# Half of the last part's q rows come through GpSimd gathers with an add instead of TensorE one-hot products

## The chip, the cores and the metric

The kernel runs on 1 core of one Trainium2 chip. The metric is the device time of one execution in microseconds (us), lower is better. Besides the plain runs, one execution was recorded by the hardware profiler; line numbers (L1119) are lines of the kernel before unless the text says otherwise.

## What is computed

A graph attention layer with 12,500 nodes of 128 values and 412,500 edges, with a norm around it. Each edge has a source, a target and 64 features:

```python
attn_in = jnp.concatenate([q[src], k[tgt], eh], axis=-1)
hmid = jax.nn.leaky_relu(attn_in @ A1 + b1, SLOPE)
scores = jax.nn.leaky_relu(hmid @ A2 + b2, SLOPE)
w = jax.nn.softmax(scores.mean(axis=-1), axis=0)      # over all edges
out = jax.ops.segment_sum(w[:, None] * v[tgt], src, num_segments=num_nodes)
y = h + out                                            # then two layer norms, with x added between
```

`q`, `k`, `v`, `h` are linear in the node features and `eh` in the edge features. `attn_in @ A1` is a sum of three terms, so the q, k and edge terms can be multiplied by A1 beforehand and added per edge.

## The kernel before

The edges come sorted by target, and the sums go by source. So the kernel sorts by itself. The 98 blocks of 128 sources each have a region in a DRAM table `rtab`, and the edges are worked through in six parts, one after the other.

*Records.* `make(p)` takes groups of 1024 edges. TensorE adds the k and v rows of the target (one-hot products with a window of `kvtab`) and the edge term in PSUM; ScalarE copies them into `rec`, a record of 260 fp32 values: 128 of k plus edge term, 128 of v, and the source's number in its block. GpSimd scatters the records, 128 rows an instruction, to the rows of `rtab` that were counted out for their blocks (L907, an indirect DMA behind a nop). This gives 3224 scatters in all.

*Sums.* `sums_of` (from L1004) works through units. A unit is two blocks, in the last part 2 x 7 = 14 tiles of 128 records, so that part has 49 units. For each unit:

- `load` (L1041): SP brings the records from `rtab` into `rt`, 1820 KB in the last four parts. There are six such buffers.
- `sources` (L1063): VectorE takes the source numbers of the records as `sl`, with the rows past the block's end masked to -1e30.
- `turn`, `turned`, `put`, `spread` (L1071, L1078, L1085, L1090): TensorE turns `sl`, VectorE makes it 8 bits (`slT`), SP writes it to DRAM (`row`) and reads it back spread to all partitions (`rowB`, 224 KB). SP's queue is in order, so it stands until `row` has landed.
- `onehot` (L1099): VectorE compares `rowB` with the partition's number: `ohT`, four tiles at a time.
- `hidden` (L1110, L1119): TensorE transposes the k rows of four tiles into the PSUM tile `ph` and adds to them the q rows of the sources, as three products (the q table `qtab` is kept as three bf16 pieces, `load_q`, L1052) with `ohT`. A unit of 14 tiles has 14 transposes and, since a chunk of four may straddle two blocks, 5 pieces x 3 = 15 products.
- `sloped`, `leaky` (L1130, L1134): ScalarE and VectorE make the leaky ReLU into `hm`; then `scores`, `heads` and the maximum follow on TensorE, and `weights` (L1219) on ScalarE.
- `select` (L1228) and `weigh` (L1242): VectorE compares `sl` with a row of block numbers, four tiles at a time (`ohs`, bf16), and ScalarE scales each tile by the edges' weights (`ohw`, fp32, two buffers).
- `add` (L1271): TensorE multiplies `ohw` with the v rows, two passes a tile, and sums over the unit's block. `total` and `store` put the block's sum beside the older parts' sums.

*The order* is written out by hand. For each unit a loop lays down a start step `s0`, a step for the load (when a buffer is free, and at least `lead` steps ahead) and, from there, the step of each function; a unit takes 8 steps. The functions of a step are issued in that order, each to its engine's queue, and each engine works in order. The sums of part p run between the steps of `make(p + 1)`; the last part's have nothing beside them. There `closing` (from L1339) already adds `beta` to the rows of `x` (`rows_x`, `moved` on GpSimd at L1357, `put_x`: 14 groups of 7 blocks). After the last unit `closing` makes the two norms, group by group.

*Tables.* In the first part `tables` (from L1502) makes `kvtab`, `qtab` and `htab` (the fp32 rows of h) between the groups: TensorE multiplies, VectorE adds the bias, ScalarE and VectorE split the sum into bf16 pieces, `own` (L1560) copies h, and `put` (L1579, L1580) writes them, 14 groups of 7 blocks.

## Time and profile before

| | |
|---|---|
| three runs | 4999.63, 5000.75 and 5002.16 us, median 5000.75 |
| profiled execution | 4997.18 us, of which the span from its first to its last instruction is 4995.4 |
| busy, share of the span | PE 84%, PEld 62%, VectorE (DVE) 80%, ScalarE (ACT) 65%, GpSimd (POOL) 66% |
| mean granted TensorE clock | 0.906 |
| moved by DMA | 1505.5 MB, mean 301 GB/s |

PE is TensorE's matmuls and PEld its weight loads, which overlap. A row of a group names line, engine and operation, the tiles written and read with their sizes and the count, then the busy time in us and the mean of one in ns, then the idle time of the engine just before them and what ended it. A row of a timeline begins with start and duration in us; in brackets at its end is the idle time ahead of it. SPq is SP issuing a DMA, not its transfer. Busy time of matmuls is modelled and neighbours overlap, so starts tell more than durations there.

### The profile page before, as it was taken

What the parts mean: (1) busy time and instruction counts of PE and PEld (TensorE: products, weight loads), DVE (VectorE), ACT (ScalarE), POOL (GpSimd) and SP (SyncE); (2) the same over time, 40 slices, a digit from 0 to 9 for tenths busy, and PEclk for the clock granted to TensorE, in tenths of its full rate; (3) what the DMA queues carried; (4) which work ended last, traced back from release to release, by engine and by line L of the source; (5) the groups of instructions that cost most, each with busy time, mean ns of one, the idle gap of its engine ahead of it and who ended that gap; (6) DMA issues with size and microseconds to landing.
All of it is one profiled execution on the core that took longest, in us unless ns stands there. A gap on an engine that the chain in (4) does not pass through costs nothing.

```text
span 4995.4 us, 98371 instructions
## 1 busy us (share of the span) xinstructions
PE 4185.0 (84%) x32676; PEld 3106.9 (62%) x32676; DVE 3984.1 (80%) x10117; ACT 3260.1 (65%) x8686; POOL 3315.9 (66%) x3268
## 2 busy tenths in 40 slices
PE   5665488898888888899999899999899999899980
PEld 3443366676566666577676676676677766667760
DVE  8886477788777777788888888888888888677778
ACT  3433266666566666677677677777777777677876
POOL 5777777777777777777777777777777777310002
PEclk7776588899999999999999899999999999999995
DMA  8999699998999988899899898989899999788763
GB/s 287 360 349 347 237 327 340 347 301 269 307 322 334 324 294 289 281 318 310 309 307 311 297 322 313 311 305 314 285 329 313 321 318 309 251 291 278 263 224 142
DMA packets 604241, 1505.50 MB, mean 301 GB/s; under 512 B 103587, under 2 KB 315702, under 8 KB 601929
## 3 DMA queue, kind: packets, MB, share of 16 engines
q1 hardware_dynamic: 448681, 1069.47, 64.9%
q0 software_dynamic: 154752, 429.39, 22.7%
q8 instruction: 259, 4.24, 0.3%
q14 instruction: 261, 2.14, 0.1%
q10 hardware_dynamic: 288, 0.26, 0.0%
HBM read 929.49 MB, written 608.37 MB: 308 GB/s over the span
## 4 chain that ended last, share of the span: by engine, by line
DMA 35%; PE 23%; DVE 15%; POOL 12%; issue 7%; ACT 6%; SPq 1%; ACTq 0%; DVEq 0%; POOLq 0%
DMA rtab<-rec,idx 17%; POOL rtab L907 12%; DMA rt<-rtab 8%; PE psm L1271 6%; DMA row<-slT 4%; PE ph L1119 4%; DMA rowB<-row 3%; PE pkv L884 3%; PE ph L1110 3%; ACT rec L895 2%; PE psc L1147 2%; DVE hm L1134 2%; PE pkv L878 2%; ACT ohw L1242 2%; PE psm L1180 2%
## 5 line engine op out<-in xcount | busy, mean ns | idle before, releaser
L907 POOL DMA_INDIRECT rtab<-rec,idx x3224 | 3253.2, 1009 | 1046.2 <-issue 778.6
L895 ACT ACTIVATE rec<-pkv 128x1024 f32<-128x1024 f32 x806 | 821.9, 1020 | 876.0 <-DMA rtab<-rec,idx 550.4
L1242 ACT ACTIVATE ohw<-ohs,w 128x128 f32<-128x128 bf16 x3822 | 1258.4, 399 | 44.7 <-DVE ohs L1228 34.3
L1271 PE MATMUL psm<-rt,ohw 128*128 128x128 f32 x7644 | 1160.2, 294 | 9.7 <-ACT ohw L1242 9.3
L1271 PEld LDWEIGHTS psm<-rt,ohw 128*128 128x128 f32 x7644 | 999.1, 200 | 58.7 <-ACT ohw L1242 16.8
L1130 ACT ACTIVATE hm<-ph 128x512 f32<-128x512 f32 (+1 forms) x1078 | 581.5, 539 | 403.9 <-PE ph L1119 399.8
L1119 PE MATMUL ph<-ohT,qs 128*128 128x256 bf16 (+3 forms) x4116 | 819.7, 321 | 0.0
L878 PE MATMUL pkv<-kvs,ohd 128*128 128x256 bf16 x3224 | 532.0, 292 | 263.4 <-ACT rec L895 252.8
L1134 DVE TENSOR_TENSOR hm<-ph,hm 128x512 f32<-128x512 f32 (+1 forms) x1078 | 668.4, 620 | 102.6 <-ACT hm L1130 101.4
L1110 PE MATMUL ph<-ident,rt 128*128 128x128 f32 x3822 | 628.1, 283 | 44.5 <-DVE hm L1134 43.2
L884 PE MATMUL pkv<-WeS,eat 64*128 64x128 f32 x6448 | 635.6, 320 | 0.0
L884 PEld LDWEIGHTS pkv<-WeS,eat 64*128 64x128 f32 x6448 | 469.8, 205 | 191.7 <-issue 187.3
L1099 DVE TENSOR_SCALAR ohT<-rowB,iotaP 128x512 bf16<-128x512 uint8 (+1 forms) x1078 | 518.7, 481 | 85.4 <-DMA rowB<-row 80.6
L878 PEld LDWEIGHTS <-ohd 128*128 128x128 bf16 x3224 | 317.1, 103 | 388.0 <-issue 298.2
L1110 PEld LDWEIGHTS ph<-ident,rt 128*128 128x128 f32 x3822 | 472.5, 152 | 62.0 <-DVE hm L1134 51.2
L1228 DVE TENSOR_TENSOR ohs<-iotaE,sl 128x512 bf16<-128x512 bf16 (+1 forms) x1078 | 430.0, 399 | 68.3 <-ACT ohw L1242 66.4
L1119 PEld LDWEIGHTS <-qs 128*128 128x128 bf16 x4116 | 396.0, 100 | 128.7 <-issue 5.1
L847 DVE TENSOR_TENSOR ats<-pc,oh 128x792 f32<-128x792 f32 x403 | 392.2, 973 | 86.6 <-PE pc L829 82.7
L1180 PE MATMUL psm<-headsum,z 128*128 128x4 f32 (+1 forms) x2156 | 285.7, 254 | 135.7 <-DVE part L1287 88.3
L1147 PE MATMUL psc<-hm,A2s 128*32 128x512 f32 (+3 forms) x2352 | 341.1, 545 | 65.7 <-DVE slT L1078 62.1
L858 DVE TENSOR_REDUCE pos<-ats 128x8 f32<-128x792 f32 x403 | 390.0, 968 | 4.0
L1180 PEld LDWEIGHTS psm<-headsum,z 128*128 128x128 f32 (+1 forms) x2156 | 280.0, 201 | 156.8 <-DVE part L1287 105.9
(175 smaller groups left out, 4082.3 us busy)
## 6 DMA issues: line engine op xcount, KB each, us to landing
rt<-rtab SPq DMA_DIRECT2D x196, 1820.0 KB
eat<-in_ea SPq DMA_DIRECT2D x201, 512.0 KB
rt<-rtab SPq DMA_DIRECT2D x49, 1560.0 KB
rt<-rtab SPq DMA_DIRECT2D x49, 1300.0 KB
qs<-qtab SPq DMA_DIRECT2D x294, 192.0 KB
rtab<-rec,idx POOLq DMA_INDIRECT x3224
dstb<-dtab SPq DMA_DIRECT2D x201, 256.0 KB
rtab<-empty SPq DMA_DIRECT2D x98, 520.0 KB
```

What stands on the lines that cost most here:

```text
L878: nc.tensor.matmul(pk[:, h, i, :], ohd[:, t * P : (t + 1) * P], kvs, start=(i == 0), stop=False,)
L884: nc.tensor.matmul(pk[:, h, i, :D], eat[h * DE : (h + 1) * DE, (j + i) * P : (j + i + 1) * P], WeS[h * DE : (h + 1) * DE, :], start=False, ...
L895: nc.scalar.activation(rec[:, :, :, : 2 * D], pk, AF.Copy)
L907: one_tile = nc.gpsimd.indirect_dma_start(out=rtab[p % TABS][:, :], out_offset=bass.IndirectOffsetOnAxis(ap=idxs[g][:, t : t + 1], axis=0) ...
L1099: nc.vector.tensor_scalar(st["oh"][k][:, : n * P], st["rowB"][:, t0 * P : (t0 + n) * P], iotaP, None, op0=ALU.is_equal,)
L1110: nc.tensor.matmul(ph[:, j * P : (j + 1) * P], st["rt"][:, t0 + j, :D], ident, is_transpose=True, start=(j == 0), stop=False,)
L1119: nc.tensor.matmul(ph[:, cols], st["qs"][:, j0 // t, s, :], oh[:, cols], start=False, stop=(s == 2 and j1 == t0 + n),)
L1130: nc.scalar.activation(hm, state[i]["ph", k][:, : n * P], AF.Copy, scale=SLOPE)
L1134: nc.vector.tensor_tensor(hm, ph[:, : n * P], hm, op=ALU.max)
L1180: nc.tensor.matmul(st["psS"][:, t0 + j : t0 + j + (nv - 1) * sw + 1 : sw], z[: 32 * nv, j * P : (j + 1) * P], headsum[: 32 * nv, :nv], sta ...
L1242: nc.scalar.activation(ohw[:, j, :], ohs[:, :, j], AF.Copy, scale=st["w"][:, t0 + j : t0 + j + 1])
L1271: nc.tensor.matmul(st["psS"][:, (1 + u) * P : (2 + u) * P], ohw[:, j, :], st["rt"][:, t0 + j, D : 2 * D], start=(k == 0), stop=(k == t - 1),)
```

## The change

In every second unit of the last part (`drawn`: 24 of the 49) the q rows are not multiplied in. VectorE clamps the source numbers to 0..127 and adds the block's first row, once per block (`rows_of`). Then GpSimd issues, tile by tile, an indirect DMA that gathers 128 rows of 512 bytes from a new DRAM table `q32` of fp32 q rows and adds them onto the k part of the records in SBUF (`draw`, 14 per unit). `hidden` only transposes. In these units `turn`, `turned`, `put`, `spread`, `load_q` and `onehot` are gone, `sources` stays five steps behind the load and the gathers come one step later; `lead` is longer by two steps. For the third four tiles of a drawn unit VectorE makes `ohw` in one operation a tile from the record's source number and the weight, in place of one `select` and four `weigh` on ScalarE. In all groups `moved` goes from GpSimd to VectorE. In the first part `own` copies q and h out of PSUM, and `put` writes `q32` in addition (448 KB a group).

```diff
+    q32 = dram.tile([nb * P, D], FP, name="q32")
...
+    first_last = NU - sum(p == NP - 1 for p, _, _ in units)
+    drawn = {i for i in range(first_last, NU) if (i - first_last) % 2 and units[i][2] <= GT}
...
             lead = turn + 8 if p in starts or p == 0 else turn + 8 + LATE
+            lead += 2 * (i in drawn)
...
+        def rows_of(i):
+            st, (p, bs, t) = state[i], units[i]
+            near = scp.tile([P, TM], FP, name="S")
+            nc.vector.tensor_scalar(
+                near[:, : len(bs) * t], st["sl"][:, : len(bs) * t], 0.0, P - 1.0,
+                op0=ALU.max, op1=ALU.min,
+            )
+            st["at"] = []
+            for u, b in enumerate(bs):
+                idx = ixp.tile([P, GT], I32, name="idx")
+                nc.vector.tensor_scalar(
+                    idx[:, :t], near[:, u * t : (u + 1) * t], float(b * P), None, op0=ALU.add
+                )
+                st["at"].append(idx)
+
+        def draw(i):
+            st, (p, bs, t) = state[i], units[i]
+            for k in range(len(bs) * t):
+                nc.gpsimd.indirect_dma_start(
+                    out=st["rt"][:, k, :D], out_offset=None, in_=q32[:, :],
+                    in_offset=bass.IndirectOffsetOnAxis(
+                        ap=st["at"][k // t][:, k % t : k % t + 1], axis=0
+                    ),
+                    compute_op=ALU.add,
+                )
...
         def hidden(i, t0, c, n, k):
-            oh = st["oh"].pop(k)
+            oh = st["oh"].pop(k, None)
...
-                    is_transpose=True, start=(j == 0), stop=False,
+                    is_transpose=True, start=(j == 0), stop=(oh is None and j == n - 1),
...
-            while j0 < t0 + n:
+            while oh is not None and j0 < t0 + n:
...
         def select(i, t0, n):
+            if i in drawn and t0 == 8:
+                ohw = st["sel"][t0] = selp.tile([P, 4, P], FP, name="ohw")
+                for j in range(n):
+                    nc.vector.tensor_scalar(
+                        ohw[:, j, :], iotaE[:, :, j], st["rt"][:, t0 + j, 2 * D : 2 * D + 1],
+                        st["w"][:, t0 + j : t0 + j + 1], op0=ALU.is_equal, op1=ALU.mult,
+                    )
+                return
...
         def weigh(i, t0, n):
+            if i in drawn and t0 == 8:
+                return
...
             do(load_at, load, i)
-            do(s0 - turn_at - 2 - e, sources, i)
-            do(s0 - turn_at, turn, i)
-            do(s0 - turn_at + 1 + e, turned, i)
-            do(s0 - turn_at + 1 + e, put, i)
-            do(s0 - turn_at + 3 + 2 * e, spread, i)
-            do(s0 - 9, load_q, i)
+            if i in drawn:
+                do(load_at + 5, sources, i)
+                do(load_at + 5, rows_of, i)
+                do(load_at + 6, draw, i)
+            else:
+...
...
-                do(s - 1 - e, onehot, i, c, n, k)
+                if i not in drawn:
+                    do(s - 1 - e, onehot, i, c, n, k)
...
         def moved(g):
-            nc.gpsimd.tensor_add(three(t, 0), three(t, 0), wide(t[:, NB * D : NB * D + D]))
+            nc.vector.tensor_add(three(t, 0), three(t, 0), wide(t[:, NB * D : NB * D + D]))
...
-                    job["h"] = np_.tile([P, NB, D], FP, name=f"h{job['i'] % 2}")
+                    job["h"] = np_.tile([P, NB, 2, D], FP, name=f"h{job['i'] % 2}")
...
         def own(job, b, m):
-            nc.scalar.activation(job["h"][:, b : b + m, :], job["ph", b][:, :, 1, :], AF.Copy)
+            nc.scalar.activation(job["h"][:, b : b + m, :, :], job["ph", b], AF.Copy)
...
-                nc.sync.dma_start(out=htab[:, bl, :], in_=job["h"])
+                nc.sync.dma_start(out=htab[:, bl, :], in_=job["h"][:, :, 1, :])
+                nc.sync.dma_start(
+                    out=q32.rearrange("(b p) d -> p b d", p=P)[:, bl, :], in_=job["h"][:, :, 0, :]
+                )
```

More of the change, by code (lines that the diff above doesn't have):

```diff
@@ L1007, in sums_of @@
         plans, s0, first, free, done, starts, ends = [], 19, None, [], [], {}, {}
-        for p, bs, t in units:
+        for i, (p, bs, t) in enumerate(units):
             nt = len(bs) * t
@@ L1299, in sums_of @@
             do(load_at, load, i)
-            do(s0 - turn_at - 2 - e, sources, i)
-            do(s0 - turn_at, turn, i)
-            do(s0 - turn_at + 1 + e, turned, i)
-            do(s0 - turn_at + 1 + e, put, i)
-            do(s0 - turn_at + 3 + 2 * e, spread, i)
-            do(s0 - 9, load_q, i)
+            if i in drawn:
[3 more added lines that the diff above has]
+            else:
+                do(s0 - turn_at - 2 - e, sources, i)
+                do(s0 - turn_at, turn, i)
+                do(s0 - turn_at + 1 + e, turned, i)
+                do(s0 - turn_at + 1 + e, put, i)
+                do(s0 - turn_at + 3 + 2 * e, spread, i)
+                do(s0 - 9, load_q, i)
             for k in range(nk):
```

## The prediction

> **What bounds the kernel now.** I began with the stages: the last scatter on GpSimd in the timeline, and the windows view, whose columns are the stretch, its length, then the busy time of PE, PEld, DVE, ACT and POOL, the granted clock, the DMA share and GB/s.
>
> ```profile
> 4302.80 0.96 POOL L907 DMA_INDIRECT rtab<-rec,idx  x1 [0.30 <-issue]
> ```
>
> ```profile
> 4313.00:4576.00 263.00, 241.31 (x1789) 181.96 (x1790) 193.49 (x520) 190.67 (x561) 29.92 (x14) 0.98 0.83 286
> 4576.00:4840.00 264.00, 262.75 (x2045) 201.62 (x2044) 203.90 (x587) 218.17 (x648) 0.00 (x0) 1.00 0.69 240
> ```
>
> GpSimd's last scatter ends at 4303.8, and the 49 units of the last part run from about 4313 to 4840, alone on the core. I call the first stretch early (the rows of x pass through it) and the second late. Late, TensorE is busy 262.75 of 264 us and ScalarE 83%, VectorE 77%, GpSimd 0. That says TensorE, but two other loops have to be read first, since they are what is left when TensorE gets less. The load of the records is issued by SP (L1041) and first read by VectorE (L1063). Here are the first and the last load of 22 in each stretch, with their reads:
>
> ```profile
> 4335.35 0.38 SPq L1041 DMA_DIRECT2D rt<-rtab  x1
> 4344.95 0.18 DVE L1063 SCALAR_TENSOR_TENSOR sl<-mask,rt 128x14 bf16<-128x14 bf16 x1 [1.77 <-DMA rt<-rtab]
> 4567.41 0.39 SPq L1041 DMA_DIRECT2D rt<-rtab  x1
> 4576.52 0.18 DVE L1063 SCALAR_TENSOR_TENSOR sl<-mask,rt 128x14 bf16<-128x14 bf16 x1 [1.15 <-DMA rt<-rtab]
> 4578.53 0.37 SPq L1041 DMA_DIRECT2D rt<-rtab  x1
> 4585.94 0.18 DVE L1063 SCALAR_TENSOR_TENSOR sl<-mask,rt 128x14 bf16<-128x14 bf16 x1 [1.09 <-DMA rt<-rtab]
> 4784.74 0.37 SPq L1041 DMA_DIRECT2D rt<-rtab  x1
> 4792.37 0.19 DVE L1063 SCALAR_TENSOR_TENSOR sl<-mask,rt 128x14 bf16<-128x14 bf16 x1 [1.33 <-DMA rt<-rtab]
> ```
>
> A unit takes (4567.41 - 4335.35)/21 = 11.05 us early and (4784.74 - 4578.53)/21 = 9.82 us late; a load takes 9.6 to 9.1 us early and 7.4 to 7.6 late, until VectorE has it. VectorE waits for it in every unit. The waits view (us in total, times, longest), the first row late, the others early:
>
> ```profile
> DVE sl L1063 <- DMA rt<-rtab: 31.7, 25, 2.2
> DVE sl L1063 <- DMA rt<-rtab: 34.1, 21, 3.0
> DVE ohT L1099 <- DMA rowB<-row: 22.3, 18, 2.9
> PE ph L1110 <- DVE hm L1134: 16.0, 15, 2.2
> ```
>
> Late, TensorE never waits for VectorE, so it is the bound. Early it does: VectorE stands behind the records, behind the source rows spread over the partitions (rowB), and behind GpSimd, as the part on VectorE shows. So the early stretch is bound by waits and the late one by TensorE, with the load close behind.
>
> **The change part by part.** *TensorE.* A unit of 14 tiles has five pieces of three products (15 matmuls, L1119) and one turn (L1071). One late unit in the timeline of PE:
>
> ```profile
> 4650.09 0.49 PE L1119 MATMUL ph<-ohT,qs 128*128 128x256 bf16 x3
> 4650.41 1.06 PE L1271 MATMUL psm<-rt,ohw 128*128 128x128 f32 x8
> 4651.90 0.81 PE L1119 MATMUL ph<-ohT,qs 128*128 128x512 bf16 x3
> 4652.64 1.06 PE L1147 MATMUL psc<-hm,A2s 128*32 128x512 f32 x8
> 4655.28 0.82 PE L1119 MATMUL ph<-ohT,qs 128*128 128x384 bf16 x6
> 4655.94 0.66 PE L1271 MATMUL psm<-rt,ohw 128*128 128x128 f32 x4
> 4656.87 0.81 PE L1119 MATMUL ph<-ohT,qs 128*128 128x512 bf16 x3
> 4657.61 0.22 PE L1071 MATMUL psc<-identB,sl 128*14 128x128 bf16 x1
> 4657.77 1.28 PE L1271 MATMUL psm<-rt,ohw 128*128 128x128 f32 x8
> ```
>
> Busy times overlap, so I go by start to next start: 0.32 + 0.74 + 0.66 + 0.74 for the products and 0.16 for the turn, 2.62 us. A drawn unit costs TensorE 9.82 - 2.62 = 7.20, and the mean of two units is 8.51. If nothing else came to bind, that is 1.31 us a unit.
>
> *GpSimd.* It gets 24 x 14 = 336 gathers with an add in the last part. No accumulating DMA stands in the trace; the nearest rows are the scatters of records (the group, then two starts in a row):
>
> ```profile
> L907 POOL DMA_INDIRECT rtab<-rec,idx x3224 | 3253.2, 1009 | 1046.2 <-issue 778.6
> 4195.75 1.03 POOL L907 DMA_INDIRECT rtab<-rec,idx  x1 [0.30 <-issue]
> 4197.09 0.96 POOL L907 DMA_INDIRECT rtab<-rec,idx  x1 [0.30 <-issue]
> ```
>
> 0.96 and 0.30 of issue are 1.27 us each, 17.8 us for a drawn unit and so 8.9 us a unit for a pair: more than TensorE's 8.51. The bounds of one gather are 0.96 (no gap, since the nop ahead of each scatter is not there) and 1.92 + 0.30 (all of it twice, if a row is fetched from two places); I take 1.27, the same number of rows in the same kind of instruction. The upper end, 31 us a pair, would cost over 250 us; the range leaves it out. By the Trainium skill, *DMA: Bandwidth & Descriptors*, "Anatomy of one DMA", many descriptors can be made before their number costs anything; by that rule the second fetch is free and the sum stays at 17.8, but no run here shows it. A gather waits for its load and its index; behind it in POOL's queue stand only later gathers, and then the closing adds. A drawn unit's products are 15 steps after its first gather, about 18 us, and the last tile is needed 6 steps later: 17.8 us and a landing fit.
>
> *The load beside the gathers.* In the late stretch the DMA engines move this much in slices of 5 us:
>
> ```profile
> GB/s 396 139 388 114 391 168 376 148 365 110 392 188 338 111 392 189 337 164 349 184 331 197 317 224 302 242 280 259 243 287 238 298 196 285 256 296 233 289 192 300
> ```
>
> They reach 390 while a load runs and fall to 110 between loads, so there is room, though not where the load is. Its 1820 KB (1.86 MB) take 4.8 of its 7.6 us at that rate. Gathers of 64 KB every 1.27 us are 52 GB/s, 13%: 0.7 us more. Half the units lose their q table and rowB (192 and 224 KB, 1.1 us at 390), 0.5 us less on average. The load becomes 7.8 us late; early, where 6.5 of 9.35 us are transfer, 9.35 + 1.0 - 0.5 = 9.85. What it bounds: the read and the slope behind it on VectorE (0.10 and 0.68) have to be over when TensorE comes to the transposes that follow the next load's issue, so a unit is not shorter than the load and 0.9 us: 8.7 late, 10.7 early.
>
> *VectorE and ScalarE.* The move of `moved` is worth more than its size. One GpSimd add of x rows, the VectorE instruction beside it, the group of that instruction late, and an operation of the added size:
>
> ```profile
> 4458.49 2.09 POOL L1357 TENSOR_TENSOR rec<-rec 128x896 f32<-128x896 f32 x1 [15.53 <-DMA rec<-in_beta]
> 4458.71 2.15 DVE L1228 TENSOR_TENSOR ohs<-iotaE,sl 128x512 bf16<-128x512 bf16 x1
> L1228 DVE TENSOR_TENSOR ohs<-iotaE,sl 128x512 bf16<-128x512 bf16 x62 | 26.1, 422 | 14.0 <-ACT ohw L1242 13.9
> L1472 DVE TENSOR_TENSOR rt<-rt,eat x14: 1057/1059/1093, 4861.4 to 4976.3; 128x896 f32<-128x896 f32 x14
> ```
>
> While GpSimd added, VectorE took 2.15 for 0.42. That stall (1.7) goes 14 times, and 1.06 us of work comes in, about 9 us less in all; the new add makes VectorE wait if the x rows are late, 0 to 2 us each. A drawn unit takes from VectorE four one-hots, the turned row and one select, and adds the clamp, two indices and four weighed one-hots:
>
> ```profile
> L1099 DVE TENSOR_SCALAR ohT<-rowB,iotaP 128x512 bf16<-128x512 uint8 x62 | 29.7, 479 | 3.7 <-DMA rowB<-row 3.7
> L1099 DVE TENSOR_SCALAR ohT<-rowB,iotaP 128x256 bf16<-128x256 uint8 x20 | 7.1, 353 | 0.3
> L1078 DVE TENSOR_SCALAR slT<-psc 14x128 uint8<-14x128 f32 x21 | 5.7, 269 | 0.0
> L1242 ACT ACTIVATE ohw<-ohs,w 128x128 f32<-128x128 bf16 x288 | 94.8, 398 | 0.6
> ```
>
> Away: 3 x 0.48 + 0.35 + 0.27 + 0.42 = 2.48. Added: three of the size of L1063 (0.18) and four of 128x128, between that and 0.35; I take 0.27: 1.6 us. VectorE gets shorter, to about 7.1 a unit, and ScalarE loses four of L1242, 0.33 each: neither becomes the bound. One new wait is real: these four write a buffer that TensorE's adds of the same step release, so VectorE stands behind TensorE, with the slope behind it, for 0 to 1 us a drawn unit; I take 0.2, 4 us in all.
>
> *SP.* Three DMAs a drawn unit go, and with them SP's wait for the row to come back; the early wait for rowB (22.3 us) halves. The plan puts two more steps between load and use; the order gets 7 steps longer, which holds no work.
>
> *The first part* writes the fp32 q rows too: 14 x 448 KB, 6.4 MB, and the copy out of PSUM doubles in size.
>
> ```profile
> 60.00:480.00 420.00, 262.19 (x1427) 174.76 (x1426) 340.22 (x746) 170.98 (x395) 311.14 (x314) 0.74 1.02 352
> 480.00:600.00 120.00, 58.53 (x343) 39.06 (x343) 63.42 (x153) 32.07 (x70) 91.09 (x91) 0.56 0.69 240
> ACT sp L1557 <- DMA qtab<-sp: 71.9, 11, 11.0
> ```
>
> There the DMA is full (1.02, 352 GB/s), so the writes are 18 us of transfer. But GpSimd sets the pace: a scatter every 1.34 us full, against 1.32 when the share is 0.69, though ScalarE stood 71.9 us behind such writes. So full DMA costs it little; between 0 and 18 I take 4.
>
> *Sum.* Late, the largest of 8.51, 8.9 and 8.7 is 8.9: 0.92 x 27 units = 25. Early 10.7: 0.35 x 24 = 8. Back come 4 and 4. That leaves 25 us. The profiled execution took 4997.2 us for a span of 4995.4, and the runs shown have a median of 5000.75; 25 off is 4972 for the one and **4976** for the other.
>
> **The rivals.** *TensorE's bound is reached* (gathers issue faster than 1.21 and the load isn't slowed): late 1.31 x 27 = 35, early as much as the wait for rowB and GpSimd's stall allow, 24: less 4, 4946. For it: the holes of 110 GB/s. Against it: the load waits of 31.7.
>
> *Every added row is fetched twice*, from the table and from the record. Then gathers take 103 of 390 GB/s, and the late transfer of 4.8 us becomes 6.5: load 7.6 + 1.7 - 0.5 = 8.8, bound 9.7, nothing gained. Early 6.5 us become 8.9: load 11.2, bound 12.1, 1 us x 24 lost. With 8 for the rest: 5030. The Trainium skill, *Collectives: The Full Stack*, "The bandwidth ceiling", has it that a reducing DMA is half as fast because it has two source reads. No run here shows an adding DMA.
>
> *The other side: GpSimd becomes the bound.* It decides from 19.64/14 = 1.40 us a gather, where a drawn unit's gathers last as long as two units do now; 0.13 us above the scatters. At 1.7 us (half of 0.96 more, for the second list of fetches) a pair takes 23.8: late 4.2 x 13.5 = 57, early 1.7 x 12 = 20, with 4 for the tables 5082. For it: POOL's total is within 10% of a pair already. Against: over 3224 scatters the mean is 1009 ns, with VectorE busy 340 of 420 us beside some of them, so little is added to an issue.
>
> *It gives nothing:* the products go, and VectorE's waits for load, x rows and adds take the time back; 5001.
>
> **How the numbers follow.** Chances: forecast 0.35, TensorE's bound 0.20, nothing 0.10, fetched twice 0.15, GpSimd 0.20. Within 0.2% is 10 us, about what a measurement of this kernel can tell from no change. Faster 0.55, same 0.10, slower 0.35. The range goes down to 4935, somewhat below TensorE's bound, and up to 5065, past the double fetch and the milder half of GpSimd's case (1.6 us a gather: 2.8 x 13.5 + 0.3 x 12 + 4 = 46). The likeliest case's own range is 4955 to 4990.
>
> **What would show it.** L1119 falls from 4116 to 3756 matmuls (24 x 15 less). The starts of the gathers: 1.27 apart is the forecast, 1.4 or more the other side, with TensorE's transposes waiting for them. The late loads: 7.8 us until VectorE reads, or 9. VectorE's instructions beside no GpSimd add should all be of normal length early. In the first part GpSimd's scatters should keep to 1.34. The forecast is wrong if a pair of late units takes over 19.6 us or if the last scatter ends more than 10 us later than 4303.8.

## The result, and the profile after

The changed kernel takes 5182.04 us (median of four runs, 5168.01 to 5189.84), against 5000.19 for the kernel before in the same session: a ratio of 1.0358, interval 1.0343 to 1.0372. It is 182 us slower, where 25 faster was forecast. In two of the sessions of the experiments the kernel before took 6142 and 6128 us, so every ratio here is to runs of before on the same chip in the same session. The profiled execution took 5168.01 us for a span of 5166.0, 170.6 us more than before's 4995.4. Line numbers are those of the changed kernel from here on: L907 is now L908, L1041 L1045, L1063 L1067, L1110 L1140, L1119 L1149, L1228 L1266, L1271 L1311, L1357 L1403, and L1090 is the new gather.

First split the 170.6 at the last scatter. It is the last row on GpSimd before the gathers (columns: start, duration, engine, line):

```profile
4340.69 0.96 POOL L908 DMA_INDIRECT rtab<-rec,idx  x1 [0.30 <-issue]
```

It ends at 4341.65, 38 us later than before's 4303.76. From there to the end are 824 us, where before had 692: 133 us more. So the loss has two places, and the larger one is the last part. There GpSimd's queue reads like this, in its timeline, and in the row of its group (busy us, mean ns, idle time ahead):

```profile
4648.66 1.54 POOL L1090 DMA_INDIRECT rt<-q,idx  x1 [0.31 <-issue]
4650.50 1.54 POOL L1090 DMA_INDIRECT rt<-q,idx  x1 [0.30 <-DMA rt<-rtab]
4652.35 1.54 POOL L1090 DMA_INDIRECT rt<-q,idx  x1 [0.30 <-issue]
```

```profile
L1090 POOL DMA_INDIRECT rt<-q,idx x336 | 530.3, 1578 | 124.3 <-issue 86.6 <-PE ph L1149 20.2 <-DVE idx L1082 2.8
```

```profile
L1090 POOL DMA_INDIRECT rt<-q,idx x336: 1533/1542/2294, 4361.9 to 4994.7; - x168
```

A gather every 1.85 us, with hardly a hole (one wait of 20 us at the start): 336 of them from 4361.9 to 4996, 634 us, of which GpSimd is busy 530 and 87 are issue. That is 26.4 us for the 14 gathers of each pair of units, which took 19.6 us late and 22.1 early before. The windows of the two halves of that stretch (columns as in the prediction) show that the other engines have more time to spare than GpSimd:

```profile
4362.00:4680.00 318.00, 252.56 (x1651) 194.59 (x1650) 197.23 (x557) 188.02 (x545) 266.76 (x169) 0.85 0.94 256
4680.00:4996.00 316.00, 243.03 (x1635) 188.13 (x1634) 183.55 (x538) 182.23 (x530) 263.15 (x168) 0.84 0.82 209
```

TensorE, busy 262.75 of 264 us in before's late stretch, is at 78% here, VectorE at 60%. TensorE's granted clock is lower too, 0.85 and 0.84 where before had 1.00 late, but with so few holes in GpSimd's queue that can't be what sets the pace. And TensorE stands for the gathers. The waits view of the same stretch (4362 to 4996):

```profile
ACT hm L1160 <- PE ph L1140: 118.0, 47, 8.3
PE ph L1140 <- DMA rt<-q,idx: 92.7, 52, 7.6
POOL rt L1090 <- issue: 86.6, 284, 0.3
DVE hm L1164 <- ACT hm L1160: 85.1, 44, 5.9
```

I read the second row as the cause, and the first and fourth as its consequence: ScalarE waits for transposes that wait for the gathers, VectorE for ScalarE. The third says that GpSimd itself hardly waits for any other engine. The loads that the prediction followed take longer as well; one of them, issue on SP and first read on VectorE:

```profile
4641.15 0.37 SPq L1045 DMA_DIRECT2D rt<-rtab  x1
4650.41 0.18 DVE L1067 SCALAR_TENSOR_TENSOR sl<-mask,rt 128x14 bf16<-128x14 bf16 x1 [4.15 <-DMA rt<-rtab]
```

9.3 us here, which is more than most: the 29 loads of this stretch that VectorE stood for by over 0.3 us take 8.7 us on average (7.5 to 12.2). The 24 like them in before's late stretch take 7.7 (7.2 to 8.5), and the forecast had 7.8.

### The profile page after: what moved, and what is told of

Read it like the earlier page. It is cut to its first block, busy times and chain, and to the rows that moved or that the text cites. A ratio compares the mean times of both kernels' runs of the same rounds, so it can differ in the third digit from the quotient of the medians.

```text
span 5166.0 us, 98225 instructions
## 1 busy us (share of the span) xinstructions
PE 4193.6 (81%) x32292; PEld 3119.0 (60%) x32292; DVE 3988.2 (77%) x10155; ACT 3242.2 (63%) x8590; POOL 3837.2 (74%) x3590
## 3 DMA queue, kind: packets, MB, share of 16 engines
q0 software_dynamic: 203136, 451.43, 25.4%
## 4 chain that ended last, share of the span: by engine, by line
DMA 39%; PE 16%; DVE 15%; POOL 14%; issue 7%; ACT 6%; SPq 1%; DVEq 0%; ACTq 0%; POOLq 0%
DMA rtab<-rec,idx 17%; POOL rtab L908 11%; DMA rt<-rtab 9%; PE psm L1311 4%; POOL rt L1090 4%; DMA rt<-q,idx 3%; DMA row<-slT 3%; PE ph L1149 2%; ACT rec L896 2%; PE pkv L885 2%; PE ph L1140 2%; DVE hm L1164 2%; PE psc L1177 2%; PE pkv L879 2%; DMA rowB<-row 2%
## 5 line engine op out<-in xcount | busy, mean ns | idle before, releaser
L908 POOL DMA_INDIRECT rtab<-rec,idx x3224 | 3274.2, 1016 | 1063.1 <-issue 792.6
L1282 ACT ACTIVATE ohw<-ohs,w 128x128 f32<-128x128 bf16 x3726 | 1227.0, 400 | 58.9 <-DVE ohs L1266 36.4
L1311 PE MATMUL psm<-rt,ohw 128*128 128x128 f32 x7644 | 1181.2, 298 | 12.4 <-ACT ohw L1282 12.0
L1311 PEld LDWEIGHTS psm<-rt,ohw 128*128 128x128 f32 x7644 | 1026.2, 205 | 64.2 <-ACT ohw L1282 24.2
L1140 PE MATMUL ph<-ident,rt 128*128 128x128 f32 x3822 | 656.5, 288 | 157.5 <-DMA rt<-q,idx 92.7
L1149 PE MATMUL ph<-ohT,qs 128*128 128x512 bf16 (+3 forms) x3756 | 757.8, 324 | 0.0
L1090 POOL DMA_INDIRECT rt<-q,idx x336 | 530.3, 1578 | 124.3 <-issue 86.6
L1140 PEld LDWEIGHTS ph<-ident,rt 128*128 128x128 f32 x3822 | 481.7, 153 | 202.0 <-DMA rt<-q,idx 82.4
L1129 DVE TENSOR_SCALAR ohT<-rowB,iotaP 128x512 bf16<-128x512 uint8 (+1 forms) x982 | 476.4, 485 | 64.0 <-DMA rowB<-row 59.0
L1266 DVE TENSOR_TENSOR ohs<-iotaE,sl 128x512 bf16<-128x512 bf16 (+1 forms) x1054 | 406.2, 385 | 76.8 <-ACT ohw L1282 76.4
L1149 PEld LDWEIGHTS <-qs 128*128 128x128 bf16 x3756 | 364.2, 101 | 120.5 <-issue 9.7
```

The costliest lines, as they stand in the source:

```text
L908: one_tile = nc.gpsimd.indirect_dma_start(out=rtab[p % TABS][:, :], out_offset=bass.IndirectOffsetOnAxis(ap=idxs[g][:, t : t + 1], axis=0) ...
L1090: nc.gpsimd.indirect_dma_start(out=st["rt"][:, k, :D], out_offset=None, in_=q32[:, :], in_offset=bass.IndirectOffsetOnAxis(ap=st["at"][k / ...
L1129: nc.vector.tensor_scalar(st["oh"][k][:, : n * P], st["rowB"][:, t0 * P : (t0 + n) * P], iotaP, None, op0=ALU.is_equal,)
L1140: nc.tensor.matmul(ph[:, j * P : (j + 1) * P], st["rt"][:, t0 + j, :D], ident, is_transpose=True, start=(j == 0), stop=(oh is None and j = ...
L1149: nc.tensor.matmul(ph[:, cols], st["qs"][:, j0 // t, s, :], oh[:, cols], start=False, stop=(s == 2 and j1 == t0 + n),)
L1282: nc.scalar.activation(ohw[:, j, :], ohs[:, :, j], AF.Copy, scale=st["w"][:, t0 + j : t0 + j + 1])
```

## The experiments

"The last stretch" is from the end of the last scatter to the end of the span: 691.6 us in before, 824.4 in the changed kernel.

Unless the text says otherwise, an edit is against the changed kernel. Where drawn units have fewer gathers, shorter ones or none, or gathers that overwrite, their sums are incomplete; such a kernel serves to measure time only.

Three theories. **One**: GpSimd's own time for an adding gather sets the pace. **Two**: the DMA engines do, which fetch each added row from two places. **Three**: the order and the waits of drawn units do (loads, indices, record buffers, VectorE).

**Half the gathers.** Each second tile of a drawn unit goes without q.

```diff
-            for k in range(len(bs) * t):
+            for k in range(0, len(bs) * t, 2):
```

> The changed kernel with 7 of each drawn unit's 14 gathers issued (every second tile; the other tiles' k part and edge term go without q). Theory one (GpSimd's own time per adding gather sets the pair of units: 14 x (1.54 + 0.30) us = 26 us): 7 x 1.85 = 13 us a pair is less than a unit pair's 19.6 us, so the stretch from the last scatter's end to the end of the span goes from 824 us back to 667-692 us and the time is 5024-5049 us. Theory two (the DMA engines, which carry each added row twice, set it): half the added rows, so much the same fall. Theory three (the drawn units' later loads, idx, ohw on VectorE and buffers set it): still about 824 us there, 5150-5180 us. This run tells three from the others.

Measured: 5056.92 us against 4998.52, ratio 1.0119 (1.0101 to 1.0137). The last stretch is 704.8 us: of the 133 us, 120 are gone. So theory three isn't the main cause; theories one and two both have room for this result. The gathers take as long as ever, but GpSimd now waits for others (260 us in its group's row, where 87 of the changed kernel's 124 are issue):

```profile
L1090 POOL DMA_INDIRECT rt<-q,idx x168 | 265.7, 1581 | 260.2 <-DVE hm L1164 59.9 <-PE psm L1311 44.8 <-issue 39.0
```

**Half the bytes.** The same number of gathers, of 256 bytes a row; the other 64 columns go without q.

```diff
-                    idx[:, :t], near[:, u * t : (u + 1) * t], float(b * P), None, op0=ALU.add
+                    idx[:, :t], near[:, u * t : (u + 1) * t], 2.0, float(2 * b * P), op0=ALU.mult, op1=ALU.add
...
-                    out=st["rt"][:, k, :D], out_offset=None, in_=q32[:, :],
+                    out=st["rt"][:, k, : D // 2], out_offset=None, in_=q32.rearrange("n (s w) -> (n s) w", s=2)[:, :],
```

> The changed kernel with each gathered row cut to its first 64 of 128 columns (256 of 512 bytes; the other columns go without q): as many instructions and descriptors, half the bytes. Theory one (GpSimd's own time, which goes by rows): gathers still 1.54 us and 1.85 us apart, 26 us a pair, 5160-5185 us. Theory two (bytes at the DMA engines): the gathers come closer together or land sooner, a pair at 20-22 us, 5080-5110 us. Theory three: 5160-5185 us with GpSimd waiting on other engines.

Measured: 5184.43, ratio 1.037 (1.0352 to 1.0387), the changed kernel's time to within the intervals. Its gathers (durations min/median/max in ns, first and last start), and the DMA queue that carries them (packets, MB, share of 16 engines) in the stretch 4600:4840, here and in the changed kernel:

```profile
L1090 POOL DMA_INDIRECT rt<-q,idx x336: 1533/1542/2366, 4363.1 to 4995.2; - x168
```

```profile
q0 software_dynamic: 18291, 4.17, 19.9%
```

```profile
q0 software_dynamic: 18415, 8.39, 28.9%
```

The bytes are halved, the DMA engines' time for them falls by a third, and the gathers stand 1.85 us apart as before. The median gather is 1542 ns in both, though the DMA engines' share between 4580 and 4840 is 0.77 here and 0.87 there. Theory one holds against two: the price is GpSimd's, and at 128 rows it does not go by bytes.

**Plain gathers.** They overwrite in place of adding, so the k part and edge term of the drawn units' sums are left out.

```diff
-                    compute_op=ALU.add,
```

> The changed kernel with its gathers overwriting in place of adding (the k part and edge term of the drawn units' hidden sums are left out), once more, as the first run of it stood on a chip where the kernel before took 6142 us. Theory one: 0.97 us a gather as in that run, 14 x 1.27 = 17.8 us a pair, under 19.6 us, last stretch 667-692 us, 5005-5049 us. Theory two: the second fetch goes, so it falls too, to 5050 us or less. Theory three: 5150-5180 us; the 1.043 of the first run of it speaks for this.

Measured: 5068.69, ratio 1.0139 (1.0122 to 1.0156). The gather's group and, for the stretch 4600:4840, its DMA queue:

```profile
L1090 POOL DMA_INDIRECT rt<-q,idx x336 | 334.6, 996 | 217.9 <-issue 91.7 <-DVE idx L1082 31.5 <-DVE ref L1239 31.1
```

```profile
q0 software_dynamic: 4877, 10.01, 13.4%
```

The add alone is 0.6 us of GpSimd per 128 rows (median 947 ns in place of 1542). It also changes what the DMA engines get: 32 packets a gather (4877 for the 154 issued there), where the adding gather has 144 (18415 for 128). In the trace the 32 are 16 of 4096 bytes and 16 of 4, the 144 are 128 of one row of 512 bytes and 16 of 4. Engine time is 13.4% of 16 x 240 us for 154 gathers, 3.3 us each, against 8.7. So an adding gather takes 2.6 times the engine time, but that is not the bound. Nor does it show a second fetch: the profile counts the same 64 KB for both kinds, and the eight times as many data packets are another possible reason, which no run separates.

But the last stretch is 724.6, still 33 us above before, with GpSimd busy for only 166 of the 260 us from 4580. What is late now? The waits of VectorE and of SP's queue, 4580 to 4840:

```profile
DVE sl L1067 <- DMA rt<-rtab: 45.5, 20, 5.9
```

```profile
SPq L1045 <- PE psm L1310: 84.9, 13, 8.8
```

SP's loads wait 6.5 us each for a record buffer that the last add of an older unit (L1310, L1311 in the changed kernel) frees. In before that row has 25.4 us in 23 waits. That became the question of the later runs.

**The tables alone.** Nothing is drawn and `moved` is on GpSimd again, so this is the kernel before with `q32` made and written.

```diff
-    drawn = {i for i in range(first_last, NU) if (i - first_last) % 2 and units[i][2] <= GT}
+    drawn = set()
...
-            nc.vector.tensor_add(three(t, 0), three(t, 0), wide(t[:, NB * D : NB * D + D]))
+            nc.gpsimd.tensor_add(three(t, 0), three(t, 0), wide(t[:, NB * D : NB * D + D]))
```

> The kernel before with the q32 table made and written in the first part, and nothing drawn from it. If the table's 6.3 MB at the first part's 348 GB/s (18 us) and ScalarE's doubled copy are what made the last scatter end 38 us later: the last scatter at 4322-4342 us, 5018-5038 us. If those 38 us come from elsewhere (scatters of 969 in place of 963 ns in kernels that hold an adding gather, 20 us): 5000-5018 us.

Measured: 5023.0, ratio 1.0042 (1.0028 to 1.0057), 24.5 us. The last scatter ends at 4331.1, 27 us late, and the last stretch is 690.2, unchanged. The hardware queue between 60 and 640 us, in before and in this kernel:

```profile
q1 hardware_dynamic: 55057, 129.91, 65.2%
```

```profile
q1 hardware_dynamic: 77085, 132.98, 68.4%
```

For 3 MB more there are 22,000 more packets. The new table's rows are 512 bytes each, 98 x 128 of them, and `htab` is now also written in pieces of 512 bytes, since `own` lays h and q side by side.

**A compact half table.** Only the 48 blocks of drawn units, their q in a tile of its own, the rows of a partition lying together; `htab` as before. Nothing is drawn, as in the run above. The part of the edit that writes the tables:

```diff
-                nc.sync.dma_start(out=htab[:, bl, :], in_=job["h"][:, :, 1, :])
-                nc.sync.dma_start(
-                    out=q32.rearrange("(b p) d -> p b d", p=P)[:, bl, :], in_=job["h"][:, :, 0, :]
-                )
+                nc.sync.dma_start(out=htab[:, bl, :], in_=job["h"])
+                if "q0" in job:
+                    q0, q1 = job["q0"], job["q1"]
+                    nc.sync.dma_start(
+                        out=q32.rearrange("(p b) d -> p b d", p=P)[:, q0:q1, :],
+                        in_=job["q"][:, : q1 - q0, :],
+                    )
```

> The kernel before with only the compact half table (48 of 98 blocks, 3.1 MB, ScalarE copying only these blocks' q) made and written, nothing drawn from it. If the whole table's 24 us are its bytes at the first part's full DMA engines (6.3 MB at 348 GB/s is 18 us): half of them, last scatter at 4314-4320, 5008-5014 us. If they are ScalarE's copies or the order of the writes, not bytes: ScalarE now has more and smaller copies, 5020-5030 us.

Measured: 5004.41, ratio 1.0009 (1.0000 to 1.0018), with the same queue:

```profile
q1 hardware_dynamic: 56974, 132.80, 66.4%
```

This is below the expectation by bytes: half the bytes cost some 4 us (interval 0 to 9), not 12. So bytes alone don't make the 24 us. The small pieces are the likely rest, but they were not tried by themselves: ScalarE's copies out of PSUM changed in this run as well.

**In the session in which before took 6142 us** four kernels ran first: plain gathers and the whole tables as above, every third unit, and the kernel before with only `moved` on VectorE. The edits of the last two (the second against the kernel before):

```diff
-    drawn = {i for i in range(first_last, NU) if (i - first_last) % 2 and units[i][2] <= GT}
+    drawn = {i for i in range(first_last, NU) if (i - first_last) % 3 == 1 and units[i][2] <= GT}
...
-            nc.gpsimd.tensor_add(three(t, 0), three(t, 0), wide(t[:, NB * D : NB * D + D]))
+            nc.vector.tensor_add(three(t, 0), three(t, 0), wide(t[:, NB * D : NB * D + D]))
```

> The changed kernel with the add left out of its gathers: the q rows overwrite the k part of the records, so that sum is left out of the result; everything else is the same, 336 gathers of 128 rows of 512 bytes. If GpSimd's own work for an add (two fetches a row) makes a gather 1.54 us, a plain one should take about 0.96, with 0.30 of issue 17.8 us a drawn unit, and the time should fall from 5182 to about 5182 - 24 x (26.4 - 19) = 5005. If the DMA engines hold the gathers back (share 0.87 in this stage), a gather that moves the same rows without fetching the record should be only a little shorter, 1.3 to 1.5 us, and the time stays above 5100. If the waits around the gathers (load, index, buffer) are the cause, the gather may be shorter but a pair of units stays near 26 us.

> The changed kernel with every third unit drawn (16 units) in place of every second. If GpSimd's issue is the bound, 14 x 1.88 = 26.4 us now cover three units, 8.8 us a unit, less than TensorE's mean of (9.82 x 2 + 7.20)/3 = 8.95; the last part would then be faster than before the change, by some 0.5 to 0.9 us for each of 49 units, and the whole, with the 38 us by which the last scatter comes later, about 4995 to 5015. If the DMA engines or VectorE's waits are the bound, the last part stays slower than before the change and the time above 5050.

> Only the first part's share of the change: q32 is written and own copies both halves, but no unit is drawn and moved stays on GpSimd. In the changed kernel the last scatter ended 38 us later (4341.7 for 4303.8). If the writes in the full stage of the first part cost this, the run is slower than before by 15 to 40 us (5015 to 5040) with the scatters behind already at 640 us; if the 6 ns by which each scatter is longer come with the table itself, about 20 of the 38 show as a longer mean of the scatter (1016 for 1009 ns) in all parts. If it was the gathers or the chip, the run equals the one before.

> Only the move of the x rows' add from GpSimd to VectorE, nothing drawn. My reading of the profile before was that each add on GpSimd stalls VectorE by 1.7 us, 14 times, against 1.06 us of work that comes in: 9 us less, 4991. The rival: VectorE waits for the x rows itself and nothing is gained, 5000 plus or minus 3, or it loses up to 15.

Measured: 1.0426 (1.0392 to 1.046), 1.0148 (1.0129 to 1.0166), 0.998 (0.9967 to 0.9993) and 0.9991 (0.9979 to 1.0004).

*Every third unit* is a miss for theory one as it stands: it expected the last part faster than before's, and the last stretch is 798 us, where the two undrawn kernels beside it have 696 and 697. GpSimd has time now (153 of 260 us busy), and TensorE waits for gathers all the same, from 5700 to 5960:

```profile
5700.00:5960.00 260.00, 206.37 (x1468) 161.02 (x1483) 158.89 (x466) 164.80 (x475) 153.22 (x98) 0.87 0.80 224
```

```profile
PE ph L1140 <- DMA rt<-q,idx: 48.5, 24, 7.6
```

So a drawn unit's 26 us of gathers can hurt in two ways: as GpSimd's total, which fills the changed kernel, and by ending after the transposes that need them, for which the prediction had left about 18 us and six steps. The second is a reading of these rows; no run gives adding gathers a longer lead, and how much of the changed kernel's loss it would make by itself is not known.

`moved` alone, worth 9 us in the prediction, gives no gain that can be told from none, but 9 us would be 0.9985 and lies in the interval too. The tables' 24 us don't show there, where the parts before the last scatter are longer anyway (it ends between 5424 and 5453 us).

The last stretch of the *plain gathers* here, 967 us against the 725 above for the same kernel, is not explained: the gathers were as short (970 ns on average, 996 above) and TensorE's granted clock was 0.74 between 5700 and 5960 us. So the last stretch of a drawn kernel from these four can't be set beside those above and below without that doubt.

**The second bound: what holds a unit up?** The runs of this part have plain gathers. First the lead of drawn units, shorter by four steps, so that a record buffer is held for less time:

```diff
-            lead += 2 * (i in drawn)
+            lead -= 2 * (i in drawn)
```

> The run with plain, overwriting gathers (k part and edge term of the drawn units left out) with a drawn unit's record buffers held shorter: its lead 20 steps in place of 24. In that run the pair of units still took 22.1 us though its gathers fill 18.2 of it, and SyncE's loads waited 6.5 us each for a buffer that the last add of an older unit frees, where before had 1.1 us. If the six record buffers, held longer by drawn units, are the second bound: these waits fall to 2-4 us, a pair to 19-20.5 us, the last stretch from 725 to 675-700 us, the time from 5069 to 5020-5045 us. If it is VectorE's early wait for the load or the order of its work: no change within 8 us. If the gathers come too late for the shorter lead: longer, with TensorE's transposes waiting on the gathers.

Measured: 5149.56, ratio 1.029 (1.0273 to 1.0307): some 75 us longer than with the long lead, by the two ratios. Only the third account had it longer, by transposes that wait for gathers, and TensorE has two such waits of 3.7 us in all between 4580 and 4840. The waits for a buffer did go (2.6 us), but SP's queue now stands elsewhere:

```profile
SPq L1114 <- DVE slT L1107: 120.0, 10, 13.3
SPq L1333 <- DVE part L1326: 57.8, 10, 7.3
SPq L1045 <- PE ph L1139: 23.1, 12, 2.9
```

The turned row of an undrawn unit is late on VectorE, which has stood for the load of a drawn unit (51.1 us in 11 waits), and behind that row in SP's queue stands the next load. That reading of the rows was not tried by itself. Next, the sources and gathers three steps later behind the load:

```diff
-                do(load_at + 5, sources, i)
-                do(load_at + 5, rows_of, i)
-                do(load_at + 6, draw, i)
+                do(load_at + 8, sources, i)
+                do(load_at + 8, rows_of, i)
+                do(load_at + 9, draw, i)
```

> The run with plain, overwriting gathers (k part and edge term of the drawn units left out), with a drawn unit's sources, indices and gathers planned three steps later after its load (8 and 9 steps in place of 5 and 6), lead 24 as there. If the rest of the loss of that run (its last stretch is 725 us, before's 692) is VectorE standing at a drawn unit's load before it has landed (45.5 us in 260, before 30.5): these waits fall to before's, the last stretch to 690-705 us, the time from 5069 to 5034-5050 us. If it is the record buffers (SyncE's loads waiting 6.5 us for one): no change within 8 us. If the gathers then come too late for TensorE: over 5075 us, with transposes waiting on gathers.

Measured: 5071.88, ratio 1.0133 (1.0114 to 1.0153), no change; VectorE's wait for the load fell from 45.5 to 13.0 us and nothing came of it (the last stretch is 734 us). It was not the bound. Then 4 plain gathers in a drawn unit, as in this edit, and none (`range(0)`; the drawn units make their indices and go without q):

```diff
-            for k in range(len(bs) * t):
+            for k in range(0, len(bs) * t, 4):
```

> The run with plain gathers (lead 24, sources 5 steps after the load), with no gather issued at all: drawn units make their indices and go without q. What is left of the change when gathers cost nothing. Theory of the buffers (six record buffers; a drawn unit's load, indices, 14 gathers and own work follow one another, so a pair of units takes a sixth of each added us more): pair 22.1 - 18.2/6 = 19.1 us in place of 22.1, 24 pairs, the last stretch from 725 to about 655 us, the time near 4996 us with the table's 24 us in it. Theory that drawn units cost by their order on VectorE and SyncE, whatever the gathers take: a pair at 21.5-22.1, 5055-5069 us.

> The same with 4 of 14 plain gathers in each drawn unit (the first tile of each four; the others go without q): 5.2 us of gathers in place of 18.2. Theory of the buffers: pair 22.1 - 13/6 = 19.9 us, last stretch about 672 us, 5015 us; the time lies on the line between none and fourteen. Theory of the order: 5055-5069 us. If only the length past some limit decides (a gather that lands after the step that needs it): as e15_none, within 8 us.

Measured, in the session in which before took 6128 us: 0.9993 (0.9976 to 1.0009) for none and 1.001 (0.9997 to 1.0023) for 4. By the length of a drawn unit's gathers, with the time of before in the same session, and with the run of the next part for a second value without gathers:

| gathers in a drawn unit | their length, us | last stretch, us | before in that session, us |
|---|---|---|---|
| none | 0 | 683 | 6128 |
| none, compact table | 0 | 678 | 5005 |
| 4 plain | 5 | 695 | 6128 |
| 7 adding | 13 | 705 | 4999 |
| 14 plain | 18 | 725 | 4999 |
| 14 plain, the unexplained run | 18 | 967 | 6142 |
| 14 adding | 26 | 824 | 5000 |

In the sessions of 5000 us the stretch grows by 47 us over the first 18 and by 99 over the next 8, where GpSimd has no time left in a pair. The row of 4 plain gathers fits, but it comes from a session of the kind in which 14 plain ones took 967. The theory of the six buffers had the growth (a sixth of each us in each of 24 pairs) but at 73 us, too large by half, and the run without gathers has the same waits for buffers (82.9 us in 16, 5700 to 5960). So buffers are not shown as the cause. What is shown is that length counts, and not order alone.

**What the idea could give at most.** No gathers, and the compact table:

> The most the idea could give: drawn units as in the run with no gather at all (they go without q), with the compact table of 48 of 98 blocks. On a chip where the kernel before takes 6128 us that run with the whole table took 6119 us, its last stretch 683 us where the run with only the table has 690-697. If the gain with free gathers is the prediction's 25 us of TensorE's time: 4978-4985 us where before takes 5000. If it is what those stretches show, 8 to 14 us, less the compact table's 3 to 6: 4988-4998 us. If drawn units cost by their order whatever the gathers take: over 5005 us.

Measured: 4997.51 against 5004.68, ratio 0.9987 (0.9977 to 0.9997): 7 us. Its last scatter ends 11 us later than before's, its last stretch is 677.9, 14 us shorter. TensorE is at 238 of 260 us late:

```profile
4580.00:4840.00 260.00, 238.00 (x1812) 187.56 (x1824) 195.57 (x594) 202.88 (x594) 0.00 (x0) 0.99 0.64 222
```

So with these units drawn and this order, gathers that cost nothing would win some 7 us (interval 2 to 12).

**Versions with the whole computation.** Plain gathers into two idle buffers and VectorE's adds, with the compact table and either lead, and every third unit with adding gathers, the compact table and the gathers three steps later:

```diff
+        def met(i, t0, n):
...
+            to = st["rt"][:, t0 : t0 + n, :D]
+            nc.vector.tensor_add(to, to, rows[:, t0 % GT : t0 % GT + n, :])
```

> The whole computation with what the runs so far point to: plain gathers (0.97 + 0.30 us) into two idle buffers, VectorE adding them to the records four tiles at a time (some 0.6 us each, 2.3 us a unit), a lead of 20 steps, the sources two steps later, and a table that holds only the drawn units' 48 of 98 blocks, in rows that lie together. If GpSimd's adding gather (13 us a pair too much), the record buffers and the table's bytes were the whole loss: last scatter at 4315-4320, last stretch 670-690, 4990-5010 us, about as before. If VectorE's adds or the gathers' lateness take the place: last stretch 710 or more, 5030 us or more.

> The whole computation with plain gathers into two idle buffers, VectorE's adds of four tiles, the compact half table, lead 24 and the gathers 9 steps after the load. Its run with lead 20 took 5165 us, with VectorE waiting 4.6 us for gathers at each add. If the short lead was its loss: as the run with plain gathers and lead 24 less 24 us of table, plus VectorE's 2.3 us a drawn unit where that engine is late: 5030-5070 us. If VectorE's adds themselves are too much: 5100 us or more. Under 5000 us if both waits go.

> The whole computation with every third unit drawn by adding gathers (16 units), its compact table of a third of the blocks, and the gathers 9 steps after the load. GpSimd's 26 us now stand against three units' 29.5 us, so theory one has GpSimd no longer the bound: last stretch 675-700 us, last scatter at 4316-4330 us (scatters 6 ns longer), 5000-5030 us. If a drawn unit costs through buffers and order whatever GpSimd does: last stretch 715 us or more, 5040 us or more.

Measured: 1.0327 (1.0313 to 1.0341), 1.0163 (1.0148 to 1.0178) and 1.0482 (1.0467 to 1.0497). The second is the best. It has the longer lead and its gathers begin one step later, and the two were not tried apart. VectorE's adds wait for gathers and TensorE for the adds even so (4580 to 4840):

```profile
PE ph L1158 <- DVE rt L1114: 33.1, 22, 4.5
DVE rt L1114 <- DMA eat<-q,idx: 28.2, 18, 3.6
```

The third is again a miss for theory one (last stretch 904 us, 675 to 700 expected): GpSimd has time there, busy 131 of 260 us, but the 26 us of gathers, begun three steps later still, end after TensorE needs them. Its waits, 4580 to 4840:

```profile
PEld ph L1145 <- DMA rt<-q,idx: 61.1, 36, 7.0
```

With the same three steps 18 us of plain gathers lost nothing that can be measured; 26 us of adding ones did not fit. No version found is faster than before.

## Why the prediction was wrong

- **The step that failed** is the term for GpSimd: "1.27 us each, 17.8 us for a drawn unit ... I take 1.27, the same number of rows in the same kind of instruction." An adding gather takes 1.54 and 0.30, 1.85 us; 14 take 25.9. The same instruction without the add does take 0.95 and 0.30. The kind of instruction was not the same.
- **The largest of three loops** failed as well. The run with plain gathers has a term of the size that was forecast, 17.8 us a drawn unit, under the 19.64 of two units; its last stretch should have been 29 us (25 + 8 - 4) shorter than before's by the prediction's sum, and it is 33 us longer. So a right GpSimd term would not have saved the forecast. That the gathers' length costs time long before GpSimd is full was not in the sum; by what wait it does is open.
- The late and early units of the sum, 27 and 24, are 51, where the part has 49; that is worth some 2 us.
- **The rival that came true** is GpSimd as the bound. Its point of decision, 1.40 us, was not tried: no run has a gather between 1.25 and 1.85. Its price, 1.7, was too low; with 1.85 the rival's own sum is (12.95 - 9.82) x 27 + (12.95 - 11.05) x 24 = 130 us, and the last stretch grew by 133. That they agree so closely is partly luck, since GpSimd's mean over the stretch is 1.89. The evidence against it (the scatters' mean) was about scatters, which don't add. I cut the range at 1.6 us a gather, though the upper bound taken from the rows was 1.92 + 0.30: the measured value lies between 1.27 and that.
- *DMA: Bandwidth & Descriptors* of the Trainium skill, "Anatomy of one DMA", by which the second fetch would be free, is not borne out for this instruction: an adding gather holds GpSimd for 1.54 us, with rows of 512 and of 256 bytes, where a plain one of 512 holds it for 0.95.
- **Every added row fetched twice** was wrong as a bound of this kernel, as half the bytes show. The DMA engines do take 8.7 against 3.3 us a gather. By the Trainium skill's *Collectives: The Full Stack*, "The bandwidth ceiling", a reducing DMA is half as fast because of its second source read; the 2.6 here agree in direction, but the packets differ too, so the reason is not shown.
- **The tables** were taken at 4 us, with 18 as the upper bound; alone they cost 24.5. The bytes were counted, the small pieces were not, and "full DMA costs it little" was wrong: scatters between 60 and 480 us fell from 314 to 304 (the row is below; 305 with the tables alone), while by the prediction they kept their pace. The small pieces may be why, as said above. The remaining 11 of the 38 us go with the adding gather, by a way that no run shows. With the whole table and nothing added, the last scatter ends at 4329 to 4337 in four kernels; with adding gathers, at 4342 to 4345 in three. With the compact table it is 4310 to 4316 in four, against 4339 in the one that adds. In all five kernels that hold an adding gather the median scatter takes 969 ns, in the others 960 to 963, and 6 ns x 3224 are 19 us.

```profile
60.00:480.00 420.00, 246.40 (x1381) 164.33 (x1381) 327.20 (x719) 173.83 (x382) 303.43 (x304) 0.76 1.02 348
```

- **VectorE's stall** went as forecast, but what that was worth is not known: the kernel with only `moved` changed leaves room for 0 and for 9 us. The one-hots of 128x512 between 4340 and 4580 have a mean of 417 ns, where before had 608 (418 in the kernel with only `moved` changed, between 5440 and 5700), and the add of `moved` takes 1.08 us there. The two rows of the one-hots, now and before, and that of the add:

```profile
L1266 DVE TENSOR_TENSOR ohs<-iotaE,sl 128x512 bf16<-128x512 bf16 x45 | 18.8, 417 | 4.4 <-ACT ohw L1282 4.4
```

```profile
L1228 DVE TENSOR_TENSOR ohs<-iotaE,sl 128x512 bf16<-128x512 bf16 x65 | 39.5, 608 | 2.9 <-ACT ohw L1242 2.9
```

```profile
L1403 DVE TENSOR_TENSOR rec<-rec 128x896 f32<-128x896 f32 x10 | 10.8, 1082 | 1.8 <-DMA rec<-in_beta 1.8
```

- **TensorE** lost its products as counted, L1149 with 3756 matmuls for 4116, but 2.62 us a drawn unit were not there to be had: without any gathers the last stretch is 7 to 14 us shorter, not 29. What else binds the drawn units at that point stays open.
- *It gives nothing* and *TensorE's bound is reached* did not come about.

## What to carry to other kernels

An indirect DMA that adds is not the plain one with an option: measure one before it is multiplied by 336, and compare the engine's own time for it with the period that it has to fit. Ask of new work not only whether its engine has time for it, but also whether it ends before it is needed: with every third unit drawn GpSimd had time and TensorE still waited. A cheaper bound engine gains only down to the next loop, so run the change with the new work left out first; here that one run would have shown that some 7 us were at stake. And a table can cost more than its bytes: look at the size of the pieces that it is written in.

## What the runs showed of the hardware

An adding gather of 128 rows holds GpSimd for 1.54 us, a plain one for 0.95 and a scatter for 0.96; with rows half as long the adding one still takes 1.54. On the DMA queue the adding gather made 128 packets of one row and 16 of 4 bytes, the plain one 16 packets of 4096 bytes and 16 of 4; the DMA engines' time was 8.7 and 3.3 us.
